# Moving pieces of due work by a step or more in a two-layer graph attention kernel

## The chip, the cores and the metric

The kernel runs on one core of a Trainium2 chip. The metric is the device time of one execution in microseconds (us), lower is better. Times inside the kernel come from one profiled execution, whose clock starts at the beginning of its span.

## What is computed

Two layers of masked attention over a graph, each with a layer norm and a ReLU ahead of it and a residual around it. There are 16 batches of 1024 nodes with 256 features, and one adjacency matrix (1024 x 1024) for each batch, which both layers use as mask. Layer 0 has 4 heads of 64, layer 1 has 8 heads of 32 (its weights are transposed and it has biases). Everything is in float32.

```python
h = jnp.maximum(_layernorm(x, axis=-1), 0.0)
x = x + _L0_gnn_ref(h, adj, Wq, Wk, Wv, Wo, bo)
h = jnp.maximum(_layernorm(x, axis=-1), 0.0)
x = x + _L1_gnn_ref(h, adj, Wq, bq, Wk, bk, Wv, bv, Wo, bo)
# each layer, with q, k, v by head:
scores = jnp.einsum('bhnd,bhmd->bhnm', q, k) / math.sqrt(D)
scores = jnp.where(adjacency == 0, -jnp.inf, scores)
w = jax.nn.softmax(scores, axis=-1)
out = jnp.einsum('bhnm,bhmd->bhnd', w, v)
return concat_of_heads(out) @ Wo.T + bo
```

## The kernel before

**Tiles and steps.** A batch of a layer is cut into two halves of 512 queries (`qh` 0 and 1) and each half into two groups of heads (`g` 0 and 1; four heads each in layer 1, two in layer 0). I write a group as (qh, g). Scores are computed transposed, with keys on the 128 partitions and the 512 queries along the free axis. A step of layer 1 is one tile of 128 keys for the four heads of a group, 8 steps a group; a step of layer 0 is two tiles of keys for two heads, 4 steps a group. So a second layer has 32 steps and a first layer 16. The order is: first layer of batch b+1, then second layer of batch b. In the code `a` is the number of the step with which the first layer of batch b+1 begins (`first[b+1]`), and `c` that of the second layer of batch b (`second[b]`), 16 steps later; the next batch's `a` is the present `c` + 32.

**What a step does.** `scores` (L531) has TensorE (PE) write the score products of a step (L539) into two PSUM pairs; a pair is two banks, and three pairs in all (`psum_pair`, L116) are shared in turn by scores, projections and output products. `exponentials` (L546) masks them on VectorE (DVE, L562, from PSUM into an SBUF tile) and takes the exponential on ScalarE (ACT, L568). `weigh` (L573) multiplies with the values on PE (L580); it runs `LEAD` = 2 steps later. Tiles of even steps come from a ring of seven (`p0`), those of odd steps are two half tiles (`p10`, `p11`) from rings of two: the half tiles of step 5 take the place of those of step 1.

**The divisors.** The sums of the softmax are counted by PE with a matrix of ones (`count`, L425). To save PE time, tiles are added before. `count_steps` (L683) has GpSimd (POOL) add an odd step's half tiles to the even step's tile (L695, two instructions), and adds pairs onto pairs with accumulating DMAs that POOL issues (`accumulate`, L681). What is left is counted some steps later. In the second layer of batch 15 (`pairs`) each pair is counted directly. `end_group` (L742) then gives the steps, counted from the group's end, at which `spread` (L442: ACT copies the sums, L445, and DMAs of SP write them one lane each), `invert` (L463: DVE takes reciprocals, L466, and SP writes them to DRAM), `fetch` (L471: SP reads them back, spread over partitions) and `normalize` (L482: POOL multiplies, L485) run, and for g = 1 `end_half` (L516), whose output product on PE is L521 and whose residual addition on DVE is L526. The last group of all (`hurry`) takes `finish` (L487) in place of this: reciprocals on DVE straight from PSUM (L505), product with the tile of heads (L506), output products (L496), residual (L511).

**The next input.** While a layer runs, the input of a later layer is prepared: `stats` (L189: DVE statistics, L198 and L199 for each of four tiles; after the last of them four small POOL instructions, L209 to L212, give 1/deviation and shift), `norm` (L214: ACT, L221), `add_bias` (L227: POOL, L230), and then the turning. `turn_blocks` (L272) transposes blocks of 32 x 32 on DVE (L273), `put_blocks` (L275) writes the tile to DRAM from SP, `place_blocks` (L280) reads it back as `hT` with four DMAs from SP. Then the projections k, q and values follow on PE, whole or in parts (L348 for a part of k or q, L307 for whole ones). `stats` can be given in two halves: tiles 0 and 1 in one step, tiles 2 and 3 with the POOL instructions in another; so `norms(inp, half, i0, i1, i2, i3)` (L856) names four steps, two for the statistics and two for the norm, and `block_inputs(inp, half, turn, put, place, k, q, values)` (L868) six.

**Order.** Nothing reorders instructions: each engine works through its own in the order in which the program names them, and `Stream.run` (L626) writes out that order by hand. At each step it issues the scores, the weighing of two steps before, the counts, then the exponentials, then what `later(i, f)` has put down for this step, with turning and large products (`rank`, L622) last. Groups of work with the same step follow in the order in which they were put down. SP and POOL each work through one queue of their own too, so a DMA waits for all that stands before it on the engine that issues it.

**What lies at the places of the change.** In a second layer of a middle batch (0 to 13) the first half's last steps and group (0,1)'s first steps carry: the second part of the statistics of the layer 1 input (`a-26`, which is `c`+6 in the second layer of the batch before), the turning of half 1 of the layer 0 input (`c`+7), the scaling of the first layer's second half (L485 on POOL, with the product L521 after it), and the additions and accumulating DMAs of group (0,0). Batch 14's second layer runs with no further first layer behind it, and carries the input of batch 15's second layer in the `else` branch at L933 to L944.

Of the kernel before, what the change touches and what calls it, by code (L numbers as in the profile page):

```python
# [10 lines left out]
F32 = mybir.dt.float32  # L11
# [7 lines left out]
P = 128  # L19
# [71 lines left out]
def fast_program(ctx, tc, a, w, loads, chk):  # L91
# [5 lines left out]
    B, N, E = x.shape  # L97
# [295 lines left out]
    class Group:  # L393
# [93 lines left out]
        def finish(self):  # L487

            inp, qh = self.inp, self.qh
            inv = work.tile([P, 512], F32, tag="inv", name=f"inv_{self.n}")  # L490
            py = psum_pair(f"py_{self.n}").rearrange("p a (t e) -> p (a t) e", e=E)
            rows, cat = xs[inp.b, qh], self.half.cat
            dst = quarters(out, inp.b, qh)

            def product(i, c):
                nc.tensor.matmul(  # L496
                    py[:, i, :], cat[:, c, ts(i, P)], w.o[self.layer][:, c, :],
                    start=c == 0 and i % 2 == 0, stop=c == 1 and i % 2 == 1,
                )

            for i in range(4):
                product(i, 0)
            for h in range(2):
                q = ts(h, 256)
                nc.vector.reciprocal(tiled(inv)[:, ts(h, 2)], by_tile(self.s)[:, ts(h, 2)])  # L505
                nc.vector.tensor_mul(cat[:, self.g, q], cat[:, self.g, q], inv[:, q])  # L506
                for i in (2 * h, 2 * h + 1):
                    product(i, 1)
            for h in range(2):
                t = ts(h, 2)  # L510
                nc.vector.tensor_add(rows[:, t, :], py[:, t, :], rows[:, t, :])  # L511
                for g in range(4):
                    queue = nc.scalar if g % 2 else nc.sync
                    queue.dma_start(dst[g][:, t, :], rows[ts(g, 32), t, :])
# [91 lines left out]
    class Stream:  # L606
# [19 lines left out]
        def run(self):  # L626
            steps = self.steps
            n = len(steps)
            waiting, i = [], 0
            while i < n + LEAD:  # L630
                wide = 2 if i < n and steps[i].gr.layer == 0 else 1
                span = range(i, i + wide)
                now = [steps[k] for k in span if k < n]
                waiting += [(k, steps[k - LEAD]) for k in span if k >= LEAD]
                for st in now:
                    scores(st)
                copies = []
                if wide == 2 or i % 2 or not self.large(i):
                    ahead = [st for _, st in waiting if st.gr.hurry and st.j >= NT - 2]
                    for _, st in waiting:  # L640
                        if st not in ahead:
                            weigh(st)
                    for k, st in waiting:
                        if st.gr.layer:
                            self.count_steps(k, st)
                        if st in ahead:
                            weigh(st)
                        if st.last:
                            copies.append(st.gr.copy_out)
                            self.end_group(k, st.gr)  # L650
                    waiting = []
                due = [self.due.pop(k, []) for k in span]

                for f, args in [e for of in due for e in of]:
                    if f.__name__ in COUNTS:
                        f(*args)
                for st in now:
                    exponentials(st, copies if wide == 1 else [])
                if not now:
                    for f in copies:  # L660
                        f()
                for k, of in zip(span, due):
                    if wide == 2 and k % 2:
                        for f in copies:
                            f()
                    if k % 2 and 3 <= k <= n and steps[k - 2].gr.layer == 0:
                        add_tiles(steps[k - 3], steps[k - 2])
                    for f, args in of:
                        if f.__name__ not in COUNTS and not self.rank((f, args)):
                            f(*args)  # L670
                for of in due:
                    for f, args in of:
                        if self.rank((f, args)):
                            f(*args)
                i += wide
            while self.due:
                for f, args in self.due.pop(min(self.due)):
                    f(*args)
# [4 lines left out]
        def count_steps(self, i, st):  # L683
# [7 lines left out]
            elif j % 2:  # L691
                one = self.steps[i - LEAD - 1].p
                for k, of in enumerate(st.halves):
                    half = one[:, ts(k, 2), :]
                    nc.gpsimd.tensor_add(half, half, of)  # L695
                if gr.pairs and (st.last or gr.hurry):
                    self.later(i + 2, gr.count, one, j == 1, st.last)
                elif gr.pairs:
                    self.halves(i + 3, gr, one, j == 1, False)
                elif j == 1:  # L700
                    gr.one = one
                elif gr.brief:
                    if j == 3:
                        self.accumulate(one, gr.one)
                        self.later(i + 6, gr.count, one, True, False)
                    elif j == 5:
                        self.halves(i + 5, gr, one, False, False)
                    else:
                        self.later(i + 4, gr.count, one, False, True)
                elif j == 5:  # L710
                    gr.two = one
                elif st.last and gr.qh and not gr.g:
                    self.accumulate(one, gr.two)
                    for k, of in enumerate((gr.one, one)):
                        self.later(i + gr.waits, gr.count, of, not k, k == 1)
                elif st.last and gr.last:
                    self.accumulate(gr.two, gr.one)
                    self.later(i + 1, self.accumulate, one, gr.two)
                    self.later(i + gr.waits, gr.count, one, True, True)
                elif st.last:  # L720
                    self.accumulate(gr.two, gr.one)
                    self.later(i + 2, self.accumulate, one, gr.two)
                    if gr.g:
                        self.halves(i + gr.waits, gr, one, True, True)
                    else:
                        self.later(i + gr.waits, gr.count, one, True, True)
                else:
                    self.accumulate(one, gr.one)
                    gr.one = one
# [12 lines left out]
        def end_group(self, i, gr):  # L742

            if gr.hurry:
                for f in (gr.spread, gr.finish, gr.inp.test):
                    self.later(i, f)
                return

# [9 lines left out]
                if gr.inp.b == 0:  # L758
                    at = (2, 3, 4, 5, 8) if gr.qh else (3, 5, 6, 7, 9)
            else:  # L760
                at = ((9, 11, 13, 19), (8, 12, 14, 17, 19), (7, 9, 11, 14), None)[2 * gr.qh + gr.g]
                if gr.pairs:
                    at = 2, 5, 6, 7, 9
                elif gr.last:
                    at = 4, 6, 7, 9, 11
            for k, f in zip(at, (gr.spread, gr.invert, gr.fetch, gr.normalize)):
# [132 lines left out]
    for b in range(B - 1):  # L899
# [5 lines left out]
            norms(mine, 1, a + 10, a + 11, a + 12, a + 13, whole=True)  # L905
            half_inputs(mine, 1, a + 15, c, c + 6, c + 2)
        else:
            norms(mine, 0, a - 27, a - 26, a - 19, a - 17, bias=a)
            block_inputs(mine, 0, a - 14, a - 11, a - 5, a, a + 2, a + 8)
            norms(mine, 1, a - 14, a - 14, a - 8, a - 6, bias=a + 6)  # L910
            block_inputs(mine, 1, a, a + 6, a + 7, c, c + (6 if b + 2 < B else 10), c + 2)
# [2 lines left out]
        if b + 2 < B:  # L914
# [3 lines left out]
            if b == 0:  # L918
                norms(other, 0, a + 12, a + 14, c, c + 1, bias=c + 34)
                block_inputs(other, 0, c + 2, c + 3, c + 4, (c + 8, c + 10), (c + 12, c + 16), c + 18)  # L920
                norms(other, 1, c + 3, c + 4, c + 6, c + 7, bias=c + 36)
                block_inputs(other, 1, c + 8, c + 9, c + 12, (c + 20, c + 22), c + 26, (c + 28, c + 30))
            else:
                norms(other, 0, a + 10, a + 12, a + 13, a + 15, bias=c + 34)
                block_inputs(other, 0, c, c + 1, c + 2, (c + 8, c + 10), (c + 12, c + 16), c + 18)
                norms(other, 1, c + 2, c + 4, c + 5, c + 6, bias=c + 36)
                block_inputs(other, 1, c + 7, c + 8, c + 12, (c + 20, c + 22), c + 26, (c + 28, c + 30))
            at = 5, 8, 10, 12, 14, 45, 49, 51, 53
            for t in range(NT):
                later(a + at[t], mask.load, t)  # L930
# [1 line left out]
                later(a + at[t + 1] + (1 if t == 4 else 2), mask.flip, t)  # L932
        else:  # L933
            last, e = inputs[1][b + 1], c + 32
            later(c + 5, last.stats, 0)
            later(c + 10, last.norm, 0)
            later(c + 13, last.add_bias, 0)
            block_inputs(last, 0, c + 11, c + 12, c + 13, c + 18, c + 22, c + 26)
            later(c + 18, last.stats, 1)
            later(c + 22, last.norm, 1)  # L940
            later(c + 23, last.add_bias, 1)
            block_inputs(last, 1, c + 23, c + 24, c + 26, e, e + 10, e + 2)
            for i, u in zip((4, 10, 14, 26, 36, 40, 42, 44), range(NT)):
                later(c + i, masks[b + 1].second, u)  # L944
    stream.run()

# [247 lines left out]
```

## Time and profile before

| | us |
|---|---|
| median of 3 runs (range) | 3082.63 (3081.44 to 3082.72) |
| profiled execution, whole | 3083.88 |
| its span | 3082.1 |
| PE busy | 3061.3 |
| POOL busy | 2462.1 |
| ACT busy | 2242.9 |
| score products L539, PE, 6144 instructions | 1089.9 |
| weighing L580, PE, 6144 instructions | 967.9 |
| masking L562, DVE, 1536 instructions | 1791.6 |
| additions L695, POOL, 510 instructions | 1218.1 |

The profile counts an engine as busy while it works on an instruction; matmuls follow each other in a pipeline, so rows of PE overlap a little. A row of the timeline gives the start, the length of the row (of several instructions in a run, their number behind an x), the engine, the line of the program, the operation, the tile written and the tiles read, and in brackets the idle time of the engine just before it, with what ended that. A line of the waits gives who waited for whom: us in total, times, the longest. In the page's list of 40 slices the granted clock of PE is 9 tenths or more everywhere.

### The profile page before, as it was taken

Reading aid. Unit: us, or ns where it says so; the run is one execution under the profiler, and the core shown is the slowest. Engines: PE = TensorE matmul, PEld = TensorE weight load, DVE = VectorE, ACT = ScalarE, POOL = GpSimd, SP = SyncE. Lnnn points to the kernel's source line nnn. Section 1 sums busy time; section 2 is a strip of 40 time slices with the busy share of each in tenths; the row PEclk is TensorE's granted clock in tenths of the full one; section 3 lists DMA queues with packets and bytes.
Section 4 is the critical chain, followed back from the end, with each engine's and each line's share of the span. In section 5 each row is a group of like instructions: output and inputs, shape, how many; then the busy total and the mean of one; then the engine's idle time right before and its main releaser. Section 6 shows DMA issues by size and latency. Waiting matters only on the chain.

```text
span 3082.1 us, 46012 instructions
## 1 busy us (share of the span) xinstructions
PE 3061.3 (99%) x16678; PEld 1199.8 (39%) x16678; DVE 2464.4 (80%) x2712; ACT 2242.9 (73%) x2478; POOL 2462.1 (80%) x1584
## 2 busy tenths in 40 slices
PE   9999999999999999999999999999999999999998
PEld 4443433434334343343433334343343433434333
DVE  6778787887878878787887878878788787887877
ACT  5668777777777767777777777777777777776775
POOL 3578788787887878878788887888878778787886
PEclk9999999999999999999999999999999999999999
DMA  4226556464563645546456463654636546463431
GB/s 134 63 61 147 129 123 135 121 141 121 129 145 110 139 130 133 136 110 138 124 129 138 120 139 108 147 123 122 141 104 144 132 122 138 118 143 86 100 82 34
DMA packets 263548, 372.77 MB, mean 121 GB/s; under 512 B 58768, under 2 KB 218768, under 8 KB 242448
## 3 DMA queue, kind: packets, MB, share of 16 engines
q0 software_dynamic: 23472, 170.93, 28.2%
q1 hardware_dynamic: 239520, 198.56, 22.2%
q8 instruction: 133, 2.18, 0.3%
q14 instruction: 103, 0.84, 0.1%
q10 hardware_dynamic: 320, 0.26, 0.0%
HBM read 149.95 MB, written 47.96 MB: 64 GB/s over the span
## 4 chain that ended last, share of the span: by engine, by line
PE 92%; DVE 2%; DMA 2%; POOL 1%; issue 1%; SPq 1%; ACT 1%; DVEq 0%; ACTq 0%; POOLq 0%
PE ps L539 31%; PE po L580 28%; PE pq L307 10%; PE py L521 7%; PE pv L383 6%; PE pq L348 5%; PE pz L425 4%; PE pv L367 2%; DVE p L562 1%; DMA p<-p 1%; POOL p L695 1%; DMA sums<-s 0%; DMA inv<-vd 0%; ACT p L568 0%; SPq L458 0%
## 5 line engine op out<-in xcount | busy, mean ns | idle before, releaser
L562 DVE SCALAR_TENSOR_TENSOR p<-mask,ps 128x1024 f32<-128x1024 fp8e5 x1536 | 1791.6, 1215 | 346.0 <-PE ps L539 327.2
L568 ACT ACTIVATE p<-p 128x1024 f32<-128x1024 f32 x1536 | 1615.9, 1056 | 597.1 <-DVE p L562 535.4
L695 POOL TENSOR_TENSOR p<-p,p 128x1024 f32<-128x1024 f32 x510 | 1218.1, 2472 | 104.9 <-PE po L580 104.3
L539 PE MATMUL ps<-qT,kT 32*128 32x512 f32 (+1 forms) x6144 | 1089.9, 629 | 5.5 <-DVE p L562 3.5
L580 PE MATMUL po<-p,v 128*32 128x512 f32 (+1 forms) x6144 | 967.9, 599 | 0.4 <-ACT cat L437 0.4
L539 PEld LDWEIGHTS ps<-qT,kT 32*128 32x128 f32 (+1 forms) x6144 | 355.4, 184 | 640.2 <-DVE p L562 269.5
L580 PEld LDWEIGHTS po<-p,v 128*32 128x32 f32 (+1 forms) x6144 | 239.4, 118 | 669.7 <-issue 498.6
L593 POOL TENSOR_TENSOR p<-p 128x1024 f32<-128x1024 f32 x128 | 302.8, 2366 | 79.4 <-DVE p L592 74.1
L592 POOL TENSOR_TENSOR p<-p,p 128x1024 f32<-128x1024 f32 x64 | 151.2, 2363 | 157.3 <-DVE p L589 128.9
L485 POOL TENSOR_TENSOR cat<-cat,inv 128x512 f32<-128x512 f32 x127 | 175.2, 1383 | 77.7 <-DMA inv<-vd 76.5
L521 PE MATMUL py<-wo,cat 128*128 128x256 f32 x1008 | 234.4, 386 | 0.0
L521 PEld LDWEIGHTS py<-wo,cat 128*128 128x128 f32 x1008 | 186.3, 190 | 73.5 <-issue 16.7
L681 POOL DMA_DIRECT2D p<-p x163 | 144.8, 889 | 86.5 <-DMA p<-p 55.2
L383 PE MATMUL pv<-wv,hT 128*128 128x256 f32 x800 | 185.7, 385 | 0.0
L307 PE MATMUL pq<-hT,wq 128*128 128x512 f32 x400 | 184.8, 605 | 0.1
L167 ACT ACTIVATE mask<-adj,numbers 128x1024 fp8e5<-128x1024 int32 x128 | 145.9, 1140 | 45.0 <-DMA adj<-in_adj_dram 45.0
L383 PEld LDWEIGHTS pv<-wv,hT 128*128 128x128 f32 x800 | 148.0, 190 | 57.1 <-issue 25.2
L589 DVE TENSOR_TENSOR p<-p 128x1024 f32<-128x1024 f32 x128 | 166.9, 1304 | 0.0
L526 DVE TENSOR_TENSOR x<-py,x 128x1024 f32<-128x1024 f32 x63 | 77.1, 1224 | 109.1 <-PE py L521 109.1
L437 ACT COPY cat<-po 128x512 f32<-128x512 f32 x128 | 73.7, 576 | 118.5 <-PE py L521 96.6
L595 POOL TENSOR_TENSOR p<-p,p 128x1024 f32<-128x1024 f32 x64 | 151.9, 2373 | 5.0
L230 POOL TENSOR_TENSOR x<-x,bo 128x1024 f32<-128x1024 f32 x64 | 155.7, 2503 | 0.0
(71 smaller groups left out, 1961.2 us busy)
## 6 DMA issues: line engine op xcount, KB each, us to landing
p<-p POOLq DMA_DIRECT2D x163, 1024.0 KB, 7.9
adj<-in_adj_dram SPq DMA_DIRECT2D x512, 128.0 KB, 3.0
turned<-hn SPq DMA_DIRECT2D x58, 512.0 KB, 3.6
hT<-turned SPq DMA_DIRECT2D x232, 128.0 KB, 2.9
x<-in_x_dram SPq DMA_DIRECT2D x128, 128.0 KB, 3.0
inv<-vd SPq DMA_DIRECT2D x128, 128.0 KB, 3.0
inv<-vd SPq DMA_DIRECT2D x252, 64.0 KB, 2.5
out_dram<-x SPq DMA_DIRECT2D x124, 128.0 KB, 2.2
```

The lines of the kernel that those rows point to most:

```text
L230: nc.gpsimd.tensor_add(rows, rows, w.bo[self.layer].unsqueeze(1).to_broadcast([P, 4, E]))
L307: nc.tensor.matmul(pq[:, m, :], wt[self.layer][:, c, ts(m, P)], self.hT[half][:, c, :], start=(c == 0), stop=(c == 1),)
L383: nc.tensor.matmul(pv[:, i, :], self.hT[half][:, c, ts(i, P)], w.v[self.layer][:, c, :], start=(c == 0), stop=(c == 1),)
L485: nc.gpsimd.tensor_mul(o, o, inv)
L521: nc.tensor.matmul(py[:, i, :], self.half.cat[:, c, ts(i, P)], w.o[self.layer][:, c, :], start=(c == 0), stop=(c == 1),)
L539: nc.tensor.matmul(st.ps[i // 2][:, i % 2, :], gr.inp.kT[r * D : (r + 1) * D, gr.g, ts(kt, P)], gr.inp.qT[gr.qh][r * D : (r + 1) * D, gr.g ...
L562: nc.vector.scalar_tensor_tensor(out=half, in0=gr.mask.m[gr.qh][:, kt // 4, :, kt % 4].unsqueeze(1).to_broadcast([P, 2, 512]), scalar=-EDG ...
L568: nc.scalar.activation(half, half, AF.Exp, scale=gr.scale)
L580: nc.tensor.matmul(gr.o[r * D : (r + 1) * D, :], gr.inp.v[:, kt, h * D : (h + 1) * D], st.halves[i // 2][:, i % 2, :], start=(kt == 0), st ...
L589: nc.vector.tensor_add(a, a, b)
L593: nc.gpsimd.tensor_add(a, a, b)
L695: nc.gpsimd.tensor_add(half, half, of)
```

## The change

Six things are changed; steps are counted as in the code.

- A: the second part of the statistics of half 0 of the layer 1 input moves from step `a-26` to `a-22`. This stands in 14 second layers (batches 0 to 13). Its POOL instructions L209 to L212 move with it: in POOL's order from before the additions of the third pair of group (0,0) to behind the accumulating DMA onto that pair and before the additions of the first pair of group (0,1).
- B: the turning and its writing for half 1 of the layer 0 input move one step later, and the reading back one step earlier (`c+7, c+8, c+12` to `c+8, c+9, c+11`; in batch 0 only the reading back moves).
- C: the inverse of group (1,0) of layer 1 moves from 9 to 10 steps after the group's end; in batch 15's group (1,0), which counts by pairs, it moves from 5 to 4.
- D: in batch 14's second layer, which prepares the input of batch 15's, statistics, norm, bias, turning, writing, reading, k and one part of the mask (`second`) move to later steps.
- E: for batch 14 (B - 2) one of the two counts of group (1,0) is done in two parts, at steps +3 and +4 after the group's end in place of +6.
- F: for the last group, the copy of the sums (`spread`) is put ahead of the copy of the weighted values and ahead of the output products; and `finish` takes its `inv` tile from the single buffer tagged `hn` in place of one of the two tagged `inv`.

```diff
@@ -487,7 +487,7 @@
         def finish(self):
 
             inp, qh = self.inp, self.qh
-            inv = work.tile([P, 512], F32, tag="inv", name=f"inv_{self.n}")
+            inv = work.tile([P, 4 * E], F32, tag="hn", bufs=1, name=f"inv_{self.n}")[:, :512]
             py = psum_pair(f"py_{self.n}").rearrange("p a (t e) -> p (a t) e", e=E)
             rows, cat = xs[inp.b, qh], self.half.cat
             dst = quarters(out, inp.b, qh)
@@ -646,6 +646,8 @@
                         if st in ahead:
                             weigh(st)
                         if st.last:
+                            if st.gr.hurry:
+                                copies.append(st.gr.spread)
                             copies.append(st.gr.copy_out)
                             self.end_group(k, st.gr)
                     waiting = []
@@ -711,8 +713,11 @@
                     gr.two = one
                 elif st.last and gr.qh and not gr.g:
                     self.accumulate(one, gr.two)
-                    for k, of in enumerate((gr.one, one)):
-                        self.later(i + gr.waits, gr.count, of, not k, k == 1)
+                    if gr.inp.b == B - 2:
+                        self.halves(i + 3, gr, gr.one, True, False)
+                    else:
+                        self.later(i + gr.waits, gr.count, gr.one, True, False)
+                    self.later(i + gr.waits, gr.count, one, False, True)
                 elif st.last and gr.last:
                     self.accumulate(gr.two, gr.one)
                     self.later(i + 1, self.accumulate, one, gr.two)
@@ -742,7 +747,7 @@
         def end_group(self, i, gr):
 
             if gr.hurry:
-                for f in (gr.spread, gr.finish, gr.inp.test):
+                for f in (gr.finish, gr.inp.test):
                     self.later(i, f)
                 return
 
@@ -758,9 +763,9 @@
                 if gr.inp.b == 0:
                     at = (2, 3, 4, 5, 8) if gr.qh else (3, 5, 6, 7, 9)
             else:
-                at = ((9, 11, 13, 19), (8, 12, 14, 17, 19), (7, 9, 11, 14), None)[2 * gr.qh + gr.g]
+                at = ((9, 11, 13, 19), (8, 12, 14, 17, 19), (7, 10, 11, 14), None)[2 * gr.qh + gr.g]
                 if gr.pairs:
-                    at = 2, 5, 6, 7, 9
+                    at = (2, 4, 5, 6, 9) if gr.qh else (2, 5, 6, 7, 9)
                 elif gr.last:
                     at = 4, 6, 7, 9, 11
             for k, f in zip(at, (gr.spread, gr.invert, gr.fetch, gr.normalize)):
@@ -905,7 +910,7 @@
             norms(mine, 1, a + 10, a + 11, a + 12, a + 13, whole=True)
             half_inputs(mine, 1, a + 15, c, c + 6, c + 2)
         else:
-            norms(mine, 0, a - 27, a - 26, a - 19, a - 17, bias=a)
+            norms(mine, 0, a - 27, a - 22, a - 19, a - 17, bias=a)
             block_inputs(mine, 0, a - 14, a - 11, a - 5, a, a + 2, a + 8)
             norms(mine, 1, a - 14, a - 14, a - 8, a - 6, bias=a + 6)
             block_inputs(mine, 1, a, a + 6, a + 7, c, c + (6 if b + 2 < B else 10), c + 2)
@@ -919,12 +924,12 @@
                 norms(other, 0, a + 12, a + 14, c, c + 1, bias=c + 34)
                 block_inputs(other, 0, c + 2, c + 3, c + 4, (c + 8, c + 10), (c + 12, c + 16), c + 18)
                 norms(other, 1, c + 3, c + 4, c + 6, c + 7, bias=c + 36)
-                block_inputs(other, 1, c + 8, c + 9, c + 12, (c + 20, c + 22), c + 26, (c + 28, c + 30))
+                block_inputs(other, 1, c + 8, c + 9, c + 11, (c + 20, c + 22), c + 26, (c + 28, c + 30))
             else:
                 norms(other, 0, a + 10, a + 12, a + 13, a + 15, bias=c + 34)
                 block_inputs(other, 0, c, c + 1, c + 2, (c + 8, c + 10), (c + 12, c + 16), c + 18)
                 norms(other, 1, c + 2, c + 4, c + 5, c + 6, bias=c + 36)
-                block_inputs(other, 1, c + 7, c + 8, c + 12, (c + 20, c + 22), c + 26, (c + 28, c + 30))
+                block_inputs(other, 1, c + 8, c + 9, c + 11, (c + 20, c + 22), c + 26, (c + 28, c + 30))
             at = 5, 8, 10, 12, 14, 45, 49, 51, 53
             for t in range(NT):
                 later(a + at[t], mask.load, t)
@@ -932,15 +937,15 @@
                 later(a + at[t + 1] + (1 if t == 4 else 2), mask.flip, t)
         else:
             last, e = inputs[1][b + 1], c + 32
-            later(c + 5, last.stats, 0)
-            later(c + 10, last.norm, 0)
-            later(c + 13, last.add_bias, 0)
-            block_inputs(last, 0, c + 11, c + 12, c + 13, c + 18, c + 22, c + 26)
-            later(c + 18, last.stats, 1)
+            later(c + 10, last.stats, 0)
+            later(c + 14, last.norm, 0)
+            later(c + 15, last.add_bias, 0)
+            block_inputs(last, 0, c + 15, c + 16, c + 17, c + 20, c + 22, c + 26)
+            later(c + 20, last.stats, 1)
             later(c + 22, last.norm, 1)
             later(c + 23, last.add_bias, 1)
             block_inputs(last, 1, c + 23, c + 24, c + 26, e, e + 10, e + 2)
-            for i, u in zip((4, 10, 14, 26, 36, 40, 42, 44), range(NT)):
+            for i, u in zip((4, 10, 20, 26, 36, 40, 42, 44), range(NT)):
                 later(c + i, masks[b + 1].second, u)
     stream.run()
```

## The prediction

> **What bounds the kernel now.** I read the page's engine shares first, then the waits, then the timelines of TensorE (PE), VectorE (DVE) and GpSimd (POOL) in the second layer of one middle batch, and at last the end of the span.
>
> ```profile
> PE 3061.3 (99%) x16678; PEld 1199.8 (39%) x16678; DVE 2464.4 (80%) x2712; ACT 2242.9 (73%) x2478; POOL 2462.1 (80%) x1584
> ...
> DVE p L562 <- POOL p L695: 6.2, 13, 1.3
> ...
> DVE inv L505 <- POOL cat L485: 5.5, 1, 5.5
> ```
>
> PE is busy 99% of 3082.1 us. A change can save only PE time that is longer than the work needs, and it loses wherever PE is made to wait. The two wait lines show POOL already holding DVE at times. I therefore compared each PE block with the usual length of its kind; the excess sums to about 41 us over the span. Two pieces recur in every middle batch, in the timeline of PE:
>
> ```profile
> 798.20 1.57 PE L539 MATMUL ps<-qT,kT 32*128 32x512 f32 x8
> ...
> 801.61 1.55 PE L539 MATMUL ps<-qT,kT 32*128 32x512 f32 x8
> ...
> 804.94 1.14 PE L539 MATMUL ps<-qT,kT 32*128 32x512 f32 x8
> ```
>
> Eight score matmuls take 1.14 us; the first two steps of group (0,1) of layer 1 take 0.43 and 0.41 more, because the PSUM pair they write is still being read by DVE. The first excess stands in 14 batches, the second in 13. DVE at that place:
>
> ```profile
> 794.84 0.42 DVE L198 BATCH_NORM_STATS2 st<-x 128x6 f32<-128x256 f32 x1
> ...
> 796.08 1.38 DVE L322 TENSOR_SCALAR qT<-pq,bq 128x512 f32<-128x512 f32 x2
> 797.37 2.34 DVE L562 SCALAR_TENSOR_TENSOR p<-mask,ps 128x1024 f32<-128x1024 fp8e5 x2
> 799.63 1.24 DVE L273 STREAM_TRANSPOSE hn<-hn 128x1024 f32<-128x1024 f32 x1
> 800.79 4.58 DVE L562 SCALAR_TENSOR_TENSOR p<-mask,ps 128x1024 f32<-128x1024 fp8e5 x4
> ```
>
> It has no gap from 788.9 to 805.4, and the statistics (794.84 to 796.16) and the turning (1.24) are in that row. POOL in the same stretch:
>
> ```profile
> 796.25 0.19 POOL L209 TENSOR_TENSOR ve<-mv,numbers 128x4 f32<-128x4 f32 x1 [0.40 <-DVE mv L199]
> ...
> 797.82 4.70 POOL L695 TENSOR_TENSOR p<-p,p 128x1024 f32<-128x1024 f32 x2
> 802.48 2.55 POOL L485 TENSOR_TENSOR cat<-cat,inv 128x512 f32<-128x512 f32 x2
> 804.97 4.71 POOL L695 TENSOR_TENSOR p<-p,p 128x1024 f32<-128x1024 f32 x2
> 809.62 0.82 POOL L681 DMA_DIRECT2D p<-p  x1
> 810.26 4.90 POOL L695 TENSOR_TENSOR p<-p,p 128x1024 f32<-128x1024 f32 x2
> 818.50 0.88 POOL L681 DMA_DIRECT2D p<-p  x1 [3.33 <-PE ps L539]
> ```
>
> POOL, too, runs back to back, from 796.25 to 815.2, and idles 3.33 only afterwards.
>
> **Parts A and B: statistics four steps later, turning one step later.** On DVE this takes 1.24 (statistics) and 1.24 (turning) out of the full stretch and puts them behind later steps, where the timeline shows DVE gaps of 0.75, 0.70 and 0.50 before L562. Batch 0, where the turning already stands one step later, has no second excess. So both PE pieces go: 14 x 0.43 + 13 x 0.41 = 11.3 us. PE would then reach the product L521 of the first layer (817.83 here, 22.56 behind the start of the last score step of group (0,0), 795.27, which I call the mark) 0.84 sooner, at 21.72.
>
> But the four POOL instructions L209 to L212 follow the statistics. They leave the head of the POOL row and, in the order of instructions, come to stand between the accumulating DMA L681 (809.62) and the additions of 810.26. Leaving the head frees little: the additions of 797.82 also wait for the PE product that reads the same tile, which reaches 797.55, and the scaling L485 behind them then waits for its divisors' DMA; at most 0.06 arrives at 804.97. Standing in the new place they cost their length. The row of batch 14, where the chain already follows L681, gives it: 2877.23 to the end of the additions' first pair takes 0.66 + 1.84 + 4.70 = 7.20 against 0.64 + 4.91 = 5.55 here, 1.65 more; the four rows at 796.25 give 1.57. I take 1.65. So the additions end at 816.8, not 815.17.
>
> Who waits for them: the second half of step 5's masked scores (L562, p_1_0_1_5_1) is written into the buffer that step 1's tile leaves, which these additions read. The batch at 1929 shows that wait, where the divisors came 1.2 later:
>
> ```profile
> 1945.63 4.98 POOL L695 TENSOR_TENSOR p<-p,p 128x1024 f32<-128x1024 f32 x2
> ...
> 1950.65 1.22 DVE L562 SCALAR_TENSOR_TENSOR p<-mask,ps 128x1024 f32<-128x1024 fp8e5 x1 [0.18 <-POOL p L695]
> ```
>
> L562 begins 0.04 behind the additions' end and lasts 1.22; the product L521 writes the PSUM pair that L562 frees, 0.05 later. So L521 begins at the additions' end + 1.65 + 1.31. Over batches 1 to 13 the additions end 19.90 to 20.28 behind the mark (21.18 once): 22.86 to 23.24 (24.14 once) against 22.56, a loss of 0.30 to 0.68 (1.58 once), together 7.3. Batch 0 (20.57 against L521 at 22.15) loses 1.4. Sum +8.7; 14 x 0.03 for the freed head leaves **+8.3**. Bounds: if step 5 had cover, -11.3; if the divisors also land 0.65 later, as in batch 0, a further 14 x 0.65 = +9.1. I take +8.3, since every link has a row. The statistics themselves end on DVE near 808.8, before POOL asks at 810.26, and L562 of step 4 is not late by more than 0.05. The DMAs of the turning: SP issues `put` a step later and `place` a step earlier, so hT's landing moves by about 2 us at most, and its first reader stands eight steps on.
>
> **Part C: the inverse of group (1,0) a step later, in batch 15 one step earlier.** L466 waited for the sums' DMA and held DVE at 1462.80 (4.45 idle before it); the next score step lost 0.68, 0.58 and 0.57 in three batches against 0.13 elsewhere. One step on, L589 and the mask's L173 (1.16 + 0.43) run before it: -1.4 (bounds 0 and -1.5). On SP the inverse's DMA now stands behind a mask load; its reader L485 comes several steps later. The short waits of pz in three batches (0.65, 1.09, 0.17) may shrink when PE comes later, or move along with it: -0.7 (bounds 0, -1.9).
>
> **Part D: batch 14's block of batch 15's input.** The statistics that fill DVE from 2873.48 to 2876.07 leave the place where one score step loses 2.35 and the next weighing 0.86. The same POOL additions that end at 2897.7 still have to pass before the products at 2899.98, and four extra count matmuls (0.1) come in. Excess in 2875 to 2953 is about 10 us, and some of it returns later: 0, bounds -3 and +2.
>
> **Part E: the tail.** The sums' copy precedes the last products, and the inverse gets the buffer tagged `hn`.
>
> ```profile
> 3066.68 1.26 POOL L485 TENSOR_TENSOR cat<-cat,inv 128x512 f32<-128x512 f32 x1 [3.05 <-DMA inv<-vd]
> ...
> 3067.98 1.76 DVE L505 RECIPROCAL inv<-pz 128x256 f32<-128x256 f32 x1 [5.47 <-POOL cat L485]
> ...
> 3072.38 1.13 PE L496 MATMUL py<-wo,cat 128*128 128x256 f32 x4 [0.94 <-DVE cat L506]
> ```
>
> The copy L445 (0.59) goes ahead of L437 and needs only the sums, so L437 at 3066.50 stays. L505 waits for L485 only through the shared buffer; it can start at about 3065.65, when the last counts end. Two times 1.76 + 0.42 then end near 3069.9, so the last products run 2.4 earlier. The check of the sums (L333, L336, L953) stands before L511 in DVE's order and moves only by the 1.3 of its DMA: **-1.8** (bounds 0, -2.4).
>
> **Sum.** +8.3 - 1.4 - 0.7 + 0 - 1.8 = +4.4. The profiled execution took 3083.88 (span 3082.1 and 1.8 around it): 3088.3 after. The median of the runs, 3082.63, is 1.25 below the profiled one, so **3087.0**.
>
> The Trainium skill ("Perfetto Trace Analysis", Optimization Strategy) says that a gap repeating on the engine that should be saturated can mean too few SBUF or PSUM buffers for the next tile. The repeated 0.43 and 0.41 are such gaps, and this change adds no buffer there; by that rule the gap would only move, which the sum above says from the rows, and by the DVE rows alone it would vanish (the first rival).
>
> **Rivals.** (1) Faster: POOL's chain is covered, and 11.3 stands. For it: 3.33 idle on POOL behind the additions, and PE's 0.84 lead. Against: the idle time lies behind the additions, not before. Time: 3082.63 - 11.3 - 1.4 - 0.7 - 1.8 = 3067.4. (2) Slower: the divisors of the scaling L485 land later beside the moved turning DMA. Batch 0 lands at 8.91 behind the mark against 8.26 to 8.64, the batch at 1929 at 9.14. All of POOL behind it moves: 14 x 0.65 is 9.1, thus about 3092 to 3096. Against: in both of those batches the request itself was issued late. It decides from 0.13 us a batch, which takes 3087.0 past 3088.8. (3) The loss on POOL only equals the 0.84 removed, and the small parts remain: 3082.63 - 3.9 = 3078.7.
>
> **Chances.** Forecast 0.50, (1) 0.25, (2) 0.15, (3) 0.10. Runs of this kernel tell 0.2% (6.2 us: 3076.4 to 3088.8) from no change. Forecast's own range is 3080 to 3094; about a third of it (0.16) is above 3088.8. Faster: 0.24 of (1), 0.02 of (3) = 0.26. Slower: 0.16 + 0.14 of (2) = 0.30. The rest, 0.44, is the same. The range goes from 3066, through half of (1), to 3094.
>
> **What would show it.** Right: score steps at 798 and 801 of 1.14 us; a PE excess of 1.1 to 1.5 at L521, its releaser DVE's L562 and before that POOL's L695; L209 at about 810.3. Wrong: L521 starting 0.8 earlier with no excess (1); additions ending more than 1.8 later (2); score steps still at 1.55, which would mean DVE is not what held them. In the tail L505 should start near 3065.7 relative to the old end.

## The result, and the profile after

The changed kernel took 3094.19 us (median of 5 runs, 3092.84 to 3097.37) beside 3082.72 for the kernel before: a ratio of 1.0038 with an interval of 1.0027 to 1.0049. It is slower by 11.5 us, where 4.4 were forecast and the range ended at 3094. Line numbers behind L648 are two higher after the change: the additions are L697, the accumulating DMAs L683.

The page's engine line, after:

```profile
PE 3056.0 (99%) x16686; PEld 1196.9 (39%) x16686; DVE 2479.0 (80%) x2712; ACT 2244.3 (73%) x2478; POOL 2462.8 (80%) x1584
```

The span is 3093.6 us, and PE was busy 5 us less than before in a span 11.5 longer: the time went into waits. The waits of the changed kernel (who waited for whom: us in total, times, longest):

```profile
POOL cat L485 <- DMA inv<-vd: 82.7, 46, 6.2
...
DVE p L562 <- POOL p L697: 32.4, 36, 4.8
...
PE py L521 <- DVE p L562: 16.2, 15, 1.2
```

DVE waited 6.2 us for the additions before and 32.4 now, and PE waits for DVE at L521 in 15 places, where it had waited nowhere.

**A middle batch.** PE's timeline in the batch whose rows at 793 to 818 were shown of before:

```profile
800.62 1.14 PE L539 MATMUL ps<-qT,kT 32*128 32x512 f32 x8
...
803.60 1.14 PE L539 MATMUL ps<-qT,kT 32*128 32x512 f32 x8
...
820.60 2.64 PE L521 MATMUL py<-wo,cat 128*128 128x256 f32 x11 [1.10 <-DVE p L562]
```

The two long score steps are 1.14 now, so 0.84 us is saved; 16 us later PE stands still for 1.10. POOL and DVE there:

```profile
799.99 4.69 POOL L697 TENSOR_TENSOR p<-p,p 128x1024 f32<-128x1024 f32 x2 [1.70 <-PE po L580]
...
812.12 0.89 POOL L683 DMA_DIRECT2D p<-p  x1
812.73 0.52 POOL L209 TENSOR_TENSOR ve<-mv,numbers 128x4 f32<-128x4 f32 x1
...
814.60 4.69 POOL L697 TENSOR_TENSOR p<-p,p 128x1024 f32<-128x1024 f32 x2
821.01 0.91 POOL L683 DMA_DIRECT2D p<-p  x1 [1.72 <-DMA p<-p]
```

```profile
816.99 1.22 DVE L562 SCALAR_TENSOR_TENSOR p<-mask,ps 128x1024 f32<-128x1024 fp8e5 x1 [0.43 <-POOL p L697]
819.32 3.48 DVE L562 SCALAR_TENSOR_TENSOR p<-mask,ps 128x1024 f32<-128x1024 fp8e5 x3 [1.11 <-POOL p L697]
```

The four small instructions (812.73 to 814.60) stand ahead of the additions; these end at 819.29, L562 begins 0.03 later, and L521 0.06 after L562's 1.22. The place that they left at the head is idle time now (1.70 at 799.99, where POOL waits for PE), and 1.72 more comes only behind the additions, too late for L562.

**Batch 14.** Here stands about half of the loss. POOL, then SP's queue, then PE:

```profile
2882.18 0.89 POOL L683 DMA_DIRECT2D p<-p  x1 [0.30 <-POOL p L697]
...
2892.15 1.15 POOL L683 DMA_DIRECT2D p<-p  x1
...
2895.59 1.27 POOL L485 TENSOR_TENSOR cat<-cat,inv 128x512 f32<-128x512 f32 x1
2900.96 1.26 POOL L485 TENSOR_TENSOR cat<-cat,inv 128x512 f32<-128x512 f32 x1 [4.10 <-DMA inv<-vd]
2902.18 4.64 POOL L697 TENSOR_TENSOR p<-p,p 128x1024 f32<-128x1024 f32 x2
```

```profile
2883.78 0.35 SPq L468 DMA_DIRECT2D vd<-vn  x1
2891.48 2.40 SPq L477 DMA_DIRECT2D inv<-vd  x4
```

```profile
2900.71 1.13 PE L539 MATMUL ps<-qT,kT 32*128 32x512 f32 x4
2905.83 2.08 PE L539 MATMUL ps<-qT,kT 32*128 32x512 f32 x4 [3.99 <-DVE p L562]
2908.14 6.51 PE L521 MATMUL py<-wo,cat 128*128 128x256 f32 x16 [0.23 <-DVE p L562]
```

The same place before the change, POOL, SP's queue and PE:

```profile
2877.23 0.89 POOL L681 DMA_DIRECT2D p<-p  x1 [0.30 <-POOL p L695]
...
2889.03 0.89 POOL L681 DMA_DIRECT2D p<-p  x1
2890.48 2.51 POOL L485 TENSOR_TENSOR cat<-cat,inv 128x512 f32<-128x512 f32 x2 [0.56 <-DMA inv<-vd]
```

```profile
2880.85 0.35 SPq L468 DMA_DIRECT2D vd<-vn  x1
2886.32 2.40 SPq L477 DMA_DIRECT2D inv<-vd  x4
```

```profile
2899.98 3.72 PE L521 MATMUL py<-wo,cat 128*128 128x256 f32 x16
```

Up to here the changed kernel was 4.9 us behind, so 4.9 has to be taken off when the two are compared. The four reads of the divisors were issued at 2891.48, 2892.01, 2892.77 and 2893.29. POOL's accumulating DMA of 1 MB came at 2892.15, between the second and the third. The first two reads landed after 3.0 us each, the others after 6.6 and 7.5, at 2900.83. Before the change the four were issued from 2886.32 to 2888.12 and that DMA at 2889.03, 0.9 us behind them. The line for L477 of the profile (min, median, max) says so, first after, then before:

```profile
DMA to landing us min/median/max: 3.0/4.8/7.5
```

```profile
DMA to landing us min/median/max: 2.9/3.1/3.5
```

The second scaling waits 4.10, the additions end at 2906.8 and L562 and PE stand still with them. After that gap PE also ran slowly: 6.51 us for L521's 16 matmuls, 3.72 before. The table of stretches (length, then busy time of PE, its weight loads PEld, DVE, ACT and POOL, each with the number of instructions in brackets, then the granted clock, DMA share and GB/s) shows the clock:

```profile
2900.00:2905.00 5.00, 1.84 (x12) 0.30 (x4) 0.45 (x1) 0.83 (x1) 4.04 (x3) 0.86 0.01 2
2905.00:2910.00 5.00, 3.94 (x8) 2.01 (x9) 3.91 (x4) 2.87 (x3) 5.00 (x4) 0.50 0.39 79
2910.00:2915.00 5.00, 5.00 (x17) 3.69 (x19) 0.66 (x2) 3.33 (x6) 3.23 (x3) 0.62 0.89 184
```

**The tail.** The timeline of its end:

```profile
3079.44 1.76 DVE L505 RECIPROCAL inv<-pz 128x256 f32<-128x256 f32 x1 [3.91 <-ACT s L445]
...
3083.91 1.13 PE L496 MATMUL py<-wo,cat 128*128 128x256 f32 x4 [1.00 <-DVE cat L506]
```

By then PE stood 13.1 us behind the old kernel; from these products on it is 11.5. L505 no longer waits for L485, but for the copy of the same sums by ACT.

### The profile page after: what moved, and what is told of

It is laid out like the page before. It is cut to its first block, busy times and chain, and to the rows that moved or that the text cites. A ratio compares the mean times of both kernels' runs of the same rounds, so it can differ in the third digit from the quotient of the medians.

```text
span 3093.6 us, 45999 instructions
## 1 busy us (share of the span) xinstructions
PE 3056.0 (99%) x16686; PEld 1196.9 (39%) x16686; DVE 2479.0 (80%) x2712; ACT 2244.3 (73%) x2478; POOL 2462.8 (80%) x1584
## 3 DMA queue, kind: packets, MB, share of 16 engines
q8 instruction: 133, 2.18, 0.3%
## 4 chain that ended last, share of the span: by engine, by line
PE 86%; POOL 6%; DVE 3%; DMA 2%; issue 1%; ACT 1%; SPq 1%; POOLq 0%; DVEq 0%; ACTq 0%
PE ps L539 28%; PE po L580 26%; PE pq L307 9%; PE py L521 7%; PE pv L383 6%; POOL p L697 5%; PE pz L425 4%; PE pq L348 3%; DVE p L562 2%; PE pv L367 2%; DMA inv<-vd 1%; ACT p L568 1%; DMA p<-p 1%; SPq L152 0%; DMA vd<-vn 0%
## 5 line engine op out<-in xcount | busy, mean ns | idle before, releaser
L562 DVE SCALAR_TENSOR_TENSOR p<-mask,ps 128x1024 f32<-128x1024 fp8e5 x1536 | 1792.3, 1215 | 348.7 <-PE ps L539 304.3
L697 POOL TENSOR_TENSOR p<-p,p 128x1024 f32<-128x1024 f32 x510 | 1213.0, 2447 | 139.2 <-PE po L580 138.5
L521 PE MATMUL py<-wo,cat 128*128 128x256 f32 x1008 | 237.2, 389 | 16.2 <-DVE p L562 16.2
L485 POOL TENSOR_TENSOR cat<-cat,inv 128x512 f32<-128x512 f32 x127 | 174.9, 1380 | 83.4 <-DMA inv<-vd 82.7
L521 PEld LDWEIGHTS py<-wo,cat 128*128 128x128 f32 x1008 | 188.2, 192 | 92.4 <-DVE p L562 30.2
L683 POOL DMA_DIRECT2D p<-p x163 | 144.1, 884 | 62.3 <-DMA p<-p 31.6
L589 DVE TENSOR_TENSOR p<-p 128x1024 f32<-128x1024 f32 x128 | 180.1, 1407 | 0.0
```

What stands on the lines that cost most here:

```text
L485: nc.gpsimd.tensor_mul(o, o, inv)
L521: nc.tensor.matmul(py[:, i, :], self.half.cat[:, c, ts(i, P)], w.o[self.layer][:, c, :], start=(c == 0), stop=(c == 1),)
L562: nc.vector.scalar_tensor_tensor(out=half, in0=gr.mask.m[gr.qh][:, kt // 4, :, kt % 4].unsqueeze(1).to_broadcast([P, 2, 512]), scalar=-EDG ...
L589: nc.vector.tensor_add(a, a, b)
```

## The experiments

Times are medians; in brackets the ratio's interval to the kernel before, which was timed beside each set of four. It took 3082.92 beside batch 14's block as before, the first run of the accumulating DMA behind the scaling, the statistics back and the statistics one step later still; 3083.65 beside the changed kernel again, the second run of that DMA, both mends and the block alone; 3083.05 beside the other four. **Batch 14's block as before** (its other lines put back too).

```diff
-            later(c + 10, last.stats, 0)
+            later(c + 5, last.stats, 0)
...
-            block_inputs(last, 0, c + 15, c + 16, c + 17, c + 20, c + 22, c + 26)
+            block_inputs(last, 0, c + 11, c + 12, c + 13, c + 18, c + 22, c + 26)
```

> Batch 14's block (part D) put back as it was before the change; everything else as changed. Theory: the changed kernel loses some 7.5 us in batch 14's second layer, because the second scaling L485 there waits 4.10 us for its divisors. Then this runs at about 3086.5, with the excess of 5.25 and 2.79 at 2900 to 2908 gone. Rival (the loss belongs to the moved inverse or to the count in two parts, which stay): 3093 to 3095.

3088.61 (1.0011 to 1.0030), and L521 in batch 14 is back at 3.72 us. So 5.6 of the 11.5 us come from this block, where 7.5 were expected. What is left, +5.7, is close to the forecast's sum, in which the block stood at nothing.

**The accumulating DMA behind the scaling**, in batch 14 only.

```diff
                 elif st.last:
-                    self.accumulate(gr.two, gr.one)
+                    d = 1 if gr.inp.b == B - 2 and not gr.qh and not gr.g else 0
+                    if d:
+                        self.later(i + 1, self.accumulate, gr.two, gr.one)
+                    else:
+                        self.accumulate(gr.two, gr.one)
```

> The changed kernel, but in batch 14 the accumulating DMA that was issued between the second and the third of the four divisor reads stands behind the scaling that waits for them. Theory (that DMA is ahead of the last two reads, which take 6.6 and 7.5 us instead of 3.0): these land near 2896.5 rather than 2900.8, the scaling waits for nothing, and the time falls by about 4 to 3090. Rival (the statistics and POOL's small chain in front of the scaling are what makes it late): the reads still land at 2899 or later, 3093 to 3095.

3092.95 (1.0020 to 1.0045): 1.2 below the changed kernel's first median, though in the profile the last read landed at 2895.56 rather than 2900.83 and the span was 4.2 shorter. The mechanism was there, its price was not settled, so it was run again beside the changed kernel.

> The changed kernel itself, beside the next three on one chip. Both theories: 3093 to 3095.

> The accumulating DMA of batch 14 behind the scaling, a second time, since the first run's profile came 4.2 shorter than the changed one and its median only 1.2. Theory (the DMA ahead of the last two divisor reads makes about half of what D costs): 2 to 5 below the changed kernel of the same call. Rival (it does so in few executions, and the chain in front is what costs): within 1.5 of it.

The changed kernel took 3095.93 (1.0025 to 1.0053), the other 3091.88 (1.0018 to 1.0039): 4.05 less, though three of its eight executions (3093.88 to 3095.86) came near the changed kernel's or among them. In the changed kernel's new profile the same DMA stood again between the second and third read, the last read took 7.4 us and L485 waited 3.51. With the DMA behind the scaling, POOL and PE read:

```profile
2896.62 2.52 POOL L485 TENSOR_TENSOR cat<-cat,inv 128x512 f32<-128x512 f32 x2
2899.08 0.89 POOL L683 DMA_DIRECT2D p<-p  x1
```

```profile
2903.69 1.13 PE L539 MATMUL ps<-qT,kT 32*128 32x512 f32 x4 [0.80 <-DVE p L562]
2905.99 3.72 PE L521 MATMUL py<-wo,cat 128*128 128x256 f32 x16 [1.17 <-DVE p L562]
```

The scaling runs without a gap, PE idles 2.0 in two pieces instead of 4.2, and L521 runs at its usual length. In the first run's profile it took 5.41 behind gaps of the same length, at a granted clock of 0.66 (2905 to 2910), which may be why the two runs put a different price on this DMA.

**Both mends in the changed kernel**: that DMA behind the scaling, and POOL's four instructions (now a function of their own, `ratios`) behind the additions.

```diff
-            later(c + 10, last.stats, 0)
+            later(c + 10, last.stats, 0, range(4), False, True)
+            later(c + 11, last.ratios, 0)
```

> The changed kernel with both mends in batch 14 (accumulating DMA behind the scaling, POOL's four instructions behind the additions). Theory: what D costs is gone but for about the 1.2 that separated the last two runs: 3088.6 + 1.2 = about 3090, 4 to 5 below the changed kernel. Rival (something else of D costs): within 2 of the changed kernel.

3090.38 (1.0011 to 1.0030), 5.55 below the changed kernel. That is 1.8 above the run with the old block, or 1.0 when each is set against its own kernel before, which the intervals do not part from nothing. PE idles 1.18 ahead of L521 (L530 in this run, whose lines stand nine further down), but it had come earlier: by the starts of the same score steps, from `c`+5 to `c`+16 this run gains 0.9 on the kernel before and the run with the old block 1.1. From `c`+16 to `c`+24 it loses 2.4 and the other 0.5. The row that the old block does not have is a wait ahead of the moved projection k:

```profile
2925.23 3.70 PE L316 MATMUL pq<-hT,wk 128*128 128x512 f32 x8 [1.19 <-DVE p L571]
```

What makes DVE late there was not tried.

**The block alone**, put into the kernel before (with the rest of its lines as in the change).

```diff
-            later(c + 5, last.stats, 0)
+            later(c + 10, last.stats, 0)
...
-            block_inputs(last, 0, c + 11, c + 12, c + 13, c + 18, c + 22, c + 26)
+            block_inputs(last, 0, c + 15, c + 16, c + 17, c + 20, c + 22, c + 26)
```

> The kernel before with batch 14's block alone moved as in the change (D). Theory (the terms add): 3082.9 + 5.6 = about 3088.5, the scaling's wait of 4 us there again. Rival (D costs only on top of the other parts): 3081 to 3084.

3089.72 (1.0010 to 1.0028), +6.1, with the wait again:

```profile
2894.26 1.26 POOL L485 TENSOR_TENSOR cat<-cat,inv 128x512 f32<-128x512 f32 x1 [3.81 <-DMA inv<-vd]
```

The block's cost does not need the other parts.

**The middle batches: statistics back at their old step**, the turning a step later kept.

```diff
-            norms(mine, 0, a - 27, a - 22, a - 19, a - 17, bias=a)
+            norms(mine, 0, a - 27, a - 26, a - 19, a - 17, bias=a)
```

> The changed kernel with the statistics of the middle batches back at their old step (part A undone, turning one step later kept). Theory (POOL's small chain in front of the additions costs the 1.2 us at L521 in each middle batch): L521 starts with no excess, the 0.41 at the second score step stays away, the 0.43 at the first returns: 3082.7 - 5.3 - 1.4 - 1.6 + 7.5 = about 3082. Rival (the moved turning makes the divisors and so the additions late): L521 keeps its excess, 3088 to 3094.

3083.36 (0.9991 to 1.0011). L521 has no excess but in batch 14 (and 0.45 in one other), and starts 22.15 us behind the mark as batch 0 did before. So the moved turning is not what makes POOL late. Less the small parts (-2.0, below) and batch 14's block (+6.1), what is left for the turning alone is about -3.7, an estimate from three runs.

**The statistics alone**, in the kernel before.

```diff
-            norms(mine, 0, a - 27, a - 26, a - 19, a - 17, bias=a)
+            norms(mine, 0, a - 27, a - 22, a - 19, a - 17, bias=a)
```

> The kernel before with only the statistics of the middle batches moved as in the change (A). Theory (L521 starts when POOL's additions let DVE free its PSUM pair, whatever PE did before): L521 stands 0.3 to 0.7 later than before in each batch and over 1.5 in batch 0, 7 to 8 in all, though the first score excess is gone and the second stays: about 3090.5. Rival (PE's own work sets L521; A only takes away 14 x 0.43): about 3077.

3090.09 (1.0011 to 1.0030), +7.0. L521 starts 22.90 to 23.21 behind the mark in batches 1 to 13 (22.56 before), whatever PE did ahead of it.

**The statistics one step later still**, batch 14's block as before.

```diff
-            norms(mine, 0, a - 27, a - 22, a - 19, a - 17, bias=a)
+            norms(mine, 0, a - 27, a - 21, a - 19, a - 17, bias=a)
```

> Statistics of the middle batches one step later still (POOL's chain then stands behind the additions that L562 waits for), and batch 14's block as before. Theory: both score excesses stay away and L521 has none: 3082.7 - 11.3 - 1.4 - 1.6 = about 3068. Rival (the chain costs wherever it stands behind the accumulating DMA, or the norm two steps on then waits for it): above 3078.

3077.62 (0.9972 to 0.9991): faster than both kernels, but 9.6 above what was expected. L521 has no excess; a new one of 0.2 to 1.0 stands at score step 5 of group (0,1) in each middle batch, 7.2 in all. PE and DVE there:

```profile
812.01 1.57 PE L539 MATMUL ps<-qT,kT 32*128 32x512 f32 x8
```

```profile
809.97 0.42 DVE L198 BATCH_NORM_STATS2 st<-x 128x6 f32<-128x256 f32 x1
...
814.04 2.34 DVE L562 SCALAR_TENSOR_TENSOR p<-mask,ps 128x1024 f32<-128x1024 fp8e5 x2
```

The good place for POOL's part is a bad one for DVE's: from 808.84, where L562 had waited 0.27 for POOL, DVE has no gap up to 816.4.

**So the two were parted**: DVE's statistics where the change puts them, POOL's four instructions a step later.

```diff
-            norms(mine, 0, a - 27, a - 22, a - 19, a - 17, bias=a)
+            later(a - 27, mine.stats, 0, (0, 1))
+            later(a - 22, mine.stats, 0, (2, 3), False, True)
+            later(a - 21, mine.ratios, 0)
+            later(a - 19, mine.norm, 0, (0, 1), False)
+            later(a - 17, mine.norm, 0, (2, 3), False)
+            later(a, mine.add_bias, 0)
```

> As the run with the statistics a step more and batch 14's block as before, but the statistics are split: the DVE part stands where the change puts it (a-22), and only POOL's four instructions stand a step later (a-21), behind the additions. Theory (the 0.37 to 0.97 that PE loses there at step 5 of group (0,1) comes from the DVE statistics at that step, 8.3 in all): that excess goes, L521 has none either, 3077.6 - 7.5 = about 3070. Rival (it comes from POOL's order): stays at 3076 to 3079.

3071.27 (0.9941 to 0.9974): 11.8 below the kernel before and some 23 below the changed one, the fastest of all. Its PE and POOL rows (again nine lines further down, L530 is the product and L218 the first of the four):

```profile
814.43 3.72 PE L530 MATMUL py<-wo,cat 128*128 128x256 f32 x16
```

```profile
807.73 5.02 POOL L706 TENSOR_TENSOR p<-p,p 128x1024 f32<-128x1024 f32 x2
812.41 0.49 POOL L218 TENSOR_TENSOR ve<-mv,numbers 128x4 f32<-128x4 f32 x1
...
815.89 0.91 POOL L692 DMA_DIRECT2D p<-p  x1 [1.58 <-DMA p<-p]
```

The four fill what was idle time behind the additions, and the product starts with no gap.

**The same with batch 14's block moved and mended twice** (the accumulating DMA as above).

```diff
-            later(c + 5, last.stats, 0)
+            later(c + 10, last.stats, 0, range(4), False, True)
+            later(c + 11, last.ratios, 0)
```

> As the run with the split, with batch 14's block as changed (D) but mended twice: the accumulating DMA behind the scaling that waits for the divisor reads, and POOL's four instructions behind the additions. Theory (the DMA and the chain in front are all that D loses, and both are gone): not slower than the run with the split, 3067 to 3071. Rival (D's statistics on DVE in their new place cost as well): 2 to 4 above it, 3072 to 3074.

3072.49 (0.9948 to 0.9976), 1.2 above the split with the old block and in the rival's range; every execution of it was slower than every one of the split. Even mended, the moved block brought nothing and cost a little. Whether DVE's statistics are the reason, as the rival says, was not tried: in the profile the product of batch 14 took 5.21 behind a gap of 1.17, against 3.72 in the split's.

**Inverses, counts and tail alone**: the change without its lines for statistics, turning and batch 14's block.

```diff
-                at = ((9, 11, 13, 19), (8, 12, 14, 17, 19), (7, 9, 11, 14), None)[2 * gr.qh + gr.g]
+                at = ((9, 11, 13, 19), (8, 12, 14, 17, 19), (7, 10, 11, 14), None)[2 * gr.qh + gr.g]
```

> The kernel before with only the moved inverses (C), the count in two parts (E) and the tail (F). Theory: -1.4 for the inverse in three batches, -1.6 for the tail as measured in the changed profile, +0.7 for new waits in batches 14 and 15 at the counts: 3082.9 - 2.3 = about 3080.5. Rival (these parts cost in batch 15 what the tail brings): 3082.5 to 3084.

3081.03 (0.9985 to 1.0004): -2.0, an effect that the interval does not part from none. The profile has the excess of the three batches at 0.12 rather than 0.57 to 0.68, as forecast, and a new wait of 1.27 at a count of batch 15.

## Why the prediction was wrong

- **Statistics and turning (+8.3 forecast).** Right in kind and size. The run with the old batch 14 block (+5.7) less the run with inverses and tail alone (-2.0) leaves +7.7. L521 was put 22.86 to 23.24 behind the mark for the batches but two; the changed profile has 22.85 to 23.22. Of the two, the batch at 1929 came earlier than said (23.22, not 24.14), because its late divisors did not recur, and batch 0 later (24.32, not 23.53; in the second profile of the changed kernel 23.38). The bound "if step 5 had cover, -11.3" came close to true in the split, which gives it that cover: -11.8, of which -2.0 are the small parts, so -9.8.
- **Inverses and tail** (the prediction's part E is F of the list). -1.4, -0.7 and -1.8 were forecast, -2.0 measured. The inverse came as said, and the tail nearly (1.6 in the changed profile), though L505 did not start with the end of the last counts, but only behind ACT's copy. The short waits of the counts did not shrink by 0.7 (1.91 before, 1.62 after, by the excess of PE's blocks), and batch 15 got a new one of about 1.
- **Batch 14's block (0 forecast, -3 to +2).** This is the step that failed: it measured +6.1 alone and +5.6 within the change. It said that "the same POOL additions that end at 2897.7 still have to pass" and followed POOL's additions, but not the DMA that POOL issues ahead of them. With the four small instructions gone from the head of its queue, POOL came to the accumulating DMA sooner: it is issued 3.1 us later in the profile than before (2892.15 against 2889.03), the reads 5.2 later (2891.48 against 2886.32), and so it went ahead of two reads that it had followed. The 4.9 taken off, the DMA came 1.8 sooner and the reads 0.3 later. The write that the reads wait for (L468) was itself issued 2.0 sooner, since DVE was free of the statistics; but that put it 1.6 us behind the accumulating DMA before it rather than 3.6, and it took 7.6 us rather than 5.4. The chain from there is in the rows: reads of 6.6 and 7.5 us, L485's wait of 4.10, additions, L562, PE. Moving that one DMA gave back 4.05 in one pair of runs and 1.2 in the other; POOL's four instructions behind the additions gave 1.5 more. The lower bound and the upper one were both taken from PE's excess and left out the DMA queue.
- **The second rival** named later divisors as what could make it slower, but laid them to the turning's DMA in the middle batches. There L485's second scaling started 8.54 behind the mark in the batch shown, against 8.45 before, and 8.48 to 8.85 in batches 1 to 13, against 8.43 to 8.77 (9.67 once), so that did not happen. What came late were the divisors of batch 14, by another DMA.
- **A price that was missing:** 2.8 us of the loss is L521 running 6.51 instead of 3.72, at a granted clock of 0.50 to 0.62 behind a gap of 3.99; in three other profiles with this block unmended it took 5.09, 5.63 and 6.10. No term of the sum had this. The Trainium skill ("TensorE: Matmul & The Clock Gate", Part 1) says that the array's clock is halved after an idle window of about 3.4 us. The traces do not agree with a whole idle window: the clock was halved 1.7 us into this gap, and in the kernel before behind a gap of 1.23 (last section).

The run with the old block (+5.7) and the block alone (+6.1) sum to 11.8, and 11.5 and 12.3 were measured for the whole change.

## What to carry to other kernels

When work leaves the head of a queue, the thing behind it goes out earlier: if that is a large DMA, look at which small reads it now overtakes, and who waits for them. A piece of work that spans two engines may need two places; here DVE's part and POOL's part, each put into its own engine's gap, turned what statistics and turning had cost (+7.7) into a gain (-9.8), with batch 14's block left where it was. Where an engine's queue is full up to a deadline, idle time behind the deadline pays for nothing.

## What was not expected of the hardware

A 1 MB accumulating DMA issued by POOL ahead of two reads of 128 KB issued by SP stretched these from about 3.0 to 6.6 and 7.5 us, and they landed with it (2900.66 for the DMA, 2899.33 and 2900.83 for the reads), although the two come from different queues. The slowest read took 7.4 to 7.7 in all four profiles with the moved block unmended; a read issued only 0.2 behind the DMA took 3.1 and 3.3 in two of them. Reads of this place with nothing of the kind ahead took about 2.8 to 3.5. The change did not bring this in: in the trace of the kernel before, 72 of the 380 reads of divisors took over 5 us, each with an accumulating DMA in flight when it was issued, and none of the 257 that were issued with none in flight took over 4.5. The Trainium skill ("DMA: Bandwidth & Descriptors", Issuing engines are not separate DMA queues) says that DMAs of all issuing engines run on the same 16 DMA engines and interleave, which fits these rows.

The granted clock fell to 0.50 around a gap of 3.99 us, and also behind one of 1.23 in the kernel before, while behind the two gaps of 0.80 and 1.17 in the runs with the DMA behind the scaling it stayed at 1.00 in one profile and fell to 0.66 (mean of 2905 to 2910) in the other. So the length of the gap alone does not tell whether the clock falls. The stretch ahead of the fall and the fall itself, first in the kernel before, then in the changed one:

```profile
2875.03:2878.44 3.41, 2.18 (x12) 0.59 (x16) 3.31 (x7) 1.07 (x2) 3.11 (x4) 1.00 0.00 0
2878.44:2881.85 3.41, 3.41 (x17) 0.64 (x16) 2.38 (x3) 3.16 (x3) 3.33 (x4) 0.50 1.06 219
```

```profile
2900.16:2903.57 3.41, 1.68 (x12) 0.30 (x4) 0.00 (x0) 0.67 (x1) 2.61 (x2) 1.00 0.00 0
2903.57:2913.81 10.24, 7.75 (x17) 5.00 (x18) 4.71 (x4) 6.19 (x8) 9.66 (x6) 0.50 0.50 102
```

The fall lasted 3.41 us in the one and three times that in the other, and in both it began a whole number of 3.413 us (842 and 849) after the clock of its execution had first risen. So where a gap lies in this raster of 3.413 us pieces seems to count beside its length: PE had been busy for 2.18 and 1.68 of the 3.41 us ahead. What decides was not tried. In eight other pieces of the raster of the changed kernel PE idled 1.10 to 1.21 with no fall behind them, and in the second run with the DMA behind the scaling one came behind 1.20, in batch 0.
